# A window-attention and spectral-mixing kernel: where in the start of the first image the weights of queries, keys and values are loaded and prepared

## The chip, the cores and the metric

The kernel runs on one core of a Trainium2 chip. The metric is device time in microseconds (us) of one execution. A core has five engines that run beside one another: TensorE (PE; its weight loads are listed apart as PEld), VectorE (DVE), ScalarE (ACT), GpSimd (POOL) and SyncE (SP, which only issues transfers here). ACT and POOL also issue transfers. All data are 32-bit floats.

## The reference, cut to what matters

The input x has 8 images of 384 channels and 64 x 64 pixels. Two layers are applied, each as x + f(group norm of x):

```python
x = x + layer0(_gn(x), ...)     # layer norm over channels, then window attention
x = x + layer1(_gn(x), ...)     # 1x1 conv, 8x8 FFT filter, 3x3 depthwise conv, gate, 1x1 conv
...
xt = (xt - mu) / jnp.sqrt(var + EPS) * norm_g + norm_b
qkv = (xt @ qkv_w + qkv_b)
```

The group norm needs the mean and variance of 32 channel groups over a whole image, so no pixel can be normalised before the whole image has been read. The layer norm then needs, for every pixel, the mean over channels and the mean of the squares. Its gain `norm_g`, its shift `norm_b` and its subtraction of the mean need not touch the pixels: they can be folded into the weights of queries, keys and values and into their biases, once per launch. What is left per pixel is one factor, 1/sqrt(var + eps).

## The kernel before, in words

Each image is cut into 8 strips of 8 pixel rows (512 pixels); a strip is a tile of 128 partitions x 3 x 512, since 384 channels are 128 partitions x 3. Per image and strip, the kernel normalises (`group_normal`, L328), squares (`ln_square`, L333), sums over channels on PE with a matrix of 1/384 (`ln_sums`), makes the factor per pixel (L347 to L352), sends it through DRAM to spread it over all partitions (L356 and L358, issued on ACT's queue for the first two strips of image 0), scales the strip (`ln_scale`, L363), and then runs the matmuls for queries and keys (`pq`), values (`pvv`), scores (`pS`), and so on.

**The squares.** `ln_square` squares all three channel thirds on ACT; POOL then adds the second and the third to the first (L335, two instructions), so that `ln_sums` needs 12 matmuls for the mean and only 4 for the squares. A matmul of 32-bit floats is two passes, so the profile shows 24 and 8.

**The order of work.** A plan lists every piece with a place in time (`at(place, piece, ...)`) and the program is written in the order of the places. PE's instructions keep exactly that order (L62), as do those handed to `keep_in_program_order`; a scheduler may move the others among themselves within an engine. `fetched` and `FETCHES` count PE's instructions, and from image 1 on `small_tiles` puts empty PE instructions in so that the runs of small 64 x 64 matmuls stand at a chosen place modulo 256.

**The start, image 0.** SP issues all 8 strips of image 0 first (L92), then the constants (L95), the two halves of the raw query and key weights (L113), the value weights `wv`, the projection weights and the rest (L119 to L123). Each transfer takes one of eight semaphores in turn, and has to wait until the last transfer with that semaphore has landed. POOL issues 64 small transfers for the position tables (L171), then clears the borders (L285, L286), and only then reaches its other work. DVE takes the statistics of each strip as it lands (`strip_stats`, L237); `input_mean` and `input_std` make the mean and the standard deviation, with one small matmul each (`pm_a`, `pv_a`).

Then the weights are prepared, in pieces that stand among the layer norm of strips 0 and 1:

- `pack_qk` (L135) copies the query and key weights into their final order, 26 blocks: 20 on DVE, 6 on POOL.
- `qk_weights(0)` and `qk_weights(1)`, one per branch: 9 matmuls `pb` fold the shift into the biases (L211, L214), then `centre`.
- `v_weights`: 12 matmuls `pv` do so for the values (L223), then `centre`.
- `centre` multiplies by the gain (L198, three instructions), sums over channels with 3 matmuls `pc`, and subtracts the mean from the weights (L202).

The first matmul that uses the result is `pq` of strip 0.

Of the kernel before, what the change touches and what calls it, by code (L numbers as in the profile page):

```python
# [9 lines left out]
ALU = mybir.AluOpType  # L10
AX = mybir.AxisListType

P = 128
KC = 3
C = 384
# [3 lines left out]
NS = SW // WS  # L19
# [19 lines left out]
def block_kernel(ctx: ExitStack, tc: tile.TileContext, out, x, consts, fsel, wqk, wv, bqk, bv,  # L39
                 wp, bp, lng, lnb, rpb1, rpb2, w_in, w_dw, w_out, filt):  # L40
    nc = tc.nc
# [8 lines left out]
    def psum(name):  # L50
        return ps.tile([P, ST], F32, tag="gemm", name=name)
# [9 lines left out]
    def matmul(*args, **kw):  # L61
        tc.keep_in_program_order(nc.tensor.matmul(*args, **kw))  # L62
        fetched["count"] += 4

        n = min(fetched["empty"], fetched["share"])
        for _ in range(n):
            tc.keep_in_program_order(nc.tensor.nop(hint="empty"))
        fetched["empty"] -= n
        fetched["count"] += n
# [5 lines left out]
    def strip(tag, bufs, name):  # L75
        return sb.tile([P, KC, ST], F32, tag=tag, bufs=bufs, name=name)

    def row512(tag, bufs, name):
        return sb.tile([P, ST], F32, tag=tag, bufs=bufs, name=name)

    def rows_of(img, s):

        return img[:, s * WS:(s + 1) * WS, :].rearrange("(p k) h w -> p k (h w)", k=KC)

    first_x = []
    for s in range(NS):
        tag, bufs = ("x", 5) if s < 5 else (("xn", 1), ("ow", 1), ("y2", 1))[s - 5]  # L90
        t = strip(tag, bufs, f"x_first{s}")
        nc.sync.dma_start(out=t, in_=rows_of(x[0], s))  # L92
        first_x.append(t)
    cst = cp.tile([P, N_CONST], F32, name="cst")
    nc.sync.dma_start(out=cst, in_=consts)  # L95
    ident = cst[:, C_ID:C_ID + P]
# [12 lines left out]
    wqk_sb = cp.tile([P, KC, 6, P], F32, name="wqk_sb")  # L109
    raw_qk = []  # L110
# [4 lines left out]
    wv_sb = cp.tile([P, KC, C], F32, name="wv_sb")  # L115
    wp_sb = cp.tile([P, KC, C], F32, name="wp_sb")
    wi_sb = cp.tile([P, KC, C], F32, name="wi_sb")
    for dst, src in ((wv_sb, wv), (wp_sb, wp), (wi_sb, w_in)):
        nc.sync.dma_start(out=dst, in_=src)  # L119
    wo_sb = cp.tile([P, 2, C], F32, name="wo_sb")  # L120
    nc.sync.dma_start(out=wo_sb[:, 0, :], in_=w_out[0:P])
# [3 lines left out]
    blocks = []  # L125
# [2 lines left out]
        blocks += [(1, 96, 16, 1, 1, 32), (1, 112, 16, 1, 1, 96)] if j == 1 else [(j, 96, 32, 1, 1, c)]  # L128
    by_branch = wqk_sb.rearrange("p k (b j) c -> p k b j c", b=2)

    def pack_qk():
        for br in range(2):
            for i, (j, to, n, t, hp, of) in enumerate(blocks):
                eng = nc.gpsimd if br and i % 2 else nc.vector
                eng.tensor_copy(by_branch[:, :, br, j, to:to + n], raw_qk[t][:, :, br, hp, of:of + n])  # L135

    vec = cp.tile([P, 18], F32, name="vec")
    lng_sb, lnb_sb = vec[:, 0:3], vec[:, 3:6]
    bqk_sb, bv_sb, bp_sb = vec[:, 6:12], vec[:, 12:15], vec[:, 15:18]
    for dst, src in ((lng_sb, lng), (lnb_sb, lnb), (bv_sb, bv), (bp_sb, bp)):  # L140
        nc.scalar.dma_start(out=dst, in_=src)
    for j, to, n, t, hp, of in blocks:
        nc.scalar.dma_start(out=bqk_sb[to:to + n].rearrange("p (b j) -> p b j", b=2)[:, :, j],
                            in_=bqk[of:of + n, 4 * t:4 * t + 4].rearrange("p (b i) -> p b i", b=2)[:, :, hp])
# [20 lines left out]
    for br, tab in ((0, rpb1), (1, rpb2)):  # L165
        raw = sb.tile([P, 2, 64], F32, tag="t2", bufs=3, name=f"rpb_raw{br}")
        raw_bias.append(raw)
        for h in range(4):
            half = slice(h % 2 * 64, h % 2 * 64 + 64)
            for y2 in range(WS):  # L170
                nc.gpsimd.dma_start(  # L171
                    out=raw[half, h // 2, y2 * WS:(y2 + 1) * WS],
                    in_=bass.AP(tab.tensor, h * 225 + y2 * 15, [[15, 8], [1, 8], [1, 8]]),
# [19 lines left out]

    bq_sb = cp.tile([P, 2, 6], F32, name="bq_sb")

    def centre(w):
        for k in range(KC):
            nc.vector.tensor_scalar(w[:, k], w[:, k], lng_sb[:, k:k + 1], None, ALU.mult)  # L198
        pc = psum("pc")
        for k in range(KC):  # L200
            matmul(pc[:, 0:C], ones_c, w[:, k], start=(k == 0), stop=(k == KC - 1))
        nc.vector.tensor_tensor(w, w, pc[:, 0:C].unsqueeze(1).to_broadcast([P, KC, C]), ALU.subtract)  # L202

    def qk_weights(br):
        pb = psum("pb")
        for j in range(3):
            for k in range(KC):
                matmul(pb[:, j:j + 1], wqk_sb[:, k, 3 * br + j, :], lnb_sb[:, k:k + 1],
                       start=(k == 0), stop=(k == KC - 1))
        own = bqk_sb[:, 3 * br:3 * br + 3]  # L210
        tc.keep_in_program_order(nc.vector.tensor_tensor(own, own, pb[:, 0:3], ALU.add))  # L211

        for i in range(2):
            nc.vector.tensor_scalar(bq_sb[:, i, 3 * br:3 * br + 3], own, pick[:, i:i + 1], None, ALU.mult)  # L214
        centre(wqk_sb[:, :, 3 * br:3 * br + 3].rearrange("p k j c -> p k (j c)"))

    def v_weights():
        pv = psum("pv")
        for lo, hi, kt, cols in ((0, P, 0, 0), (0, 64, 1, 192), (64, P, 1, 128), (0, P, 2, 256)):
            for k in range(KC):  # L220
                matmul(pv[lo:hi, kt:kt + 1], wv_sb[:, k, cols:cols + hi - lo], lnb_sb[:, k:k + 1],
                       start=(k == 0), stop=(k == KC - 1))
        nc.vector.tensor_tensor(bv_sb, bv_sb, pv[:, 0:3], ALU.add)  # L223
        centre(wv_sb)

    def out_bias():
        pp = psum("pp")
# [49 lines left out]
    def at(place, piece, *args):  # L277
        plan.append((place, len(plan), piece, args))

    xs, ys, y2s, qks, vs, os_, ots, x1s, zs = ({} for _ in range(9))  # L280
# [21 lines left out]
    def load(b, s, what):  # L302

        if b == 0 and (what == "stats" or what == "norm" and s < 3):
            xs[b, s, what] = first_x[s]
            return
        t = xs[b, s, what] = strip("x", 5, f"x_{what}_{b}_{s}")
        src = x1d[b][s] if what in ("mix", "finish") else rows_of(x[b], s)
        in_dense_work(nc.sync.dma_start(out=t, in_=src))
# [13 lines left out]
    def group_normal(b, s):  # L323
# [3 lines left out]
        for k in range(KC):  # L327
            nc.vector.tensor_scalar(by_window(y[:, k, :]), image_order(t[:, k, :]), gs[:, 0:1], gs[:, 1:2],  # L328
                                    ALU.subtract, ALU.mult)

    def ln_square(b, s):
        sq = ys[b, s, "sq"] = strip("sq", 1, f"sq_{b}_{s}")
        nc.scalar.activation(sq, ys[b, s], AF.Square)  # L333
        for k in (1, 2):
            nc.gpsimd.tensor_tensor(sq[:, 0, :], sq[:, 0, :], sq[:, k, :], ALU.add)  # L335

    def ln_sums(b, s):


        p = psum(f"ln_{b}_{s}")  # L340
        for to, t, n in ((0, ys[b, s], KC), (P, ys.pop((b, s, "sq")), 1)):
            for k in range(n):
                for j in range(4):
                    matmul(p[32 * j:32 * (j + 1), to:to + P], ones_c[:, 0:32], t[:, k, j * P:(j + 1) * P],
                           start=(k == 0), stop=(k == n - 1))
        m = sb.tile([P, 2 * P], F32, tag="lc", bufs=1, name=f"m_{b}_{s}")
        nc.scalar.copy(m, p[:, 0:2 * P])  # L347
        rc = sb.tile([P, P], F32, tag="lr", bufs=2, name=f"lr_{b}_{s}")
        nc.vector.tensor_tensor(rc, m[:, 0:P], m[:, 0:P], ALU.mult)  # L349
        nc.vector.tensor_tensor(rc, m[:, P:2 * P], rc, ALU.subtract)  # L350
        nc.scalar.activation(rc, rc, AF.Sqrt, bias=eps_t)
        nc.vector.reciprocal(rc, rc)  # L352

        line = dr.tile([4, P], F32, tag="line", bufs=4, name=f"line_{b}_{s}")
        queue = nc.scalar if b == 0 and s < 2 else nc.sync
        queue.dma_start(out=line, in_=rc[0:P:32, :])  # L356
        rs = ys[b, s, "rs"] = row512("rs", 2, f"rs_{b}_{s}")
        queue.dma_start(out=rs, in_=bass.AP(line.tensor, line.offset, [[0, P], [1, ST]]))  # L358
# [354 lines left out]
    for b in range(B):  # L713
# [4 lines left out]
            at(u, load, b, s, "stats")  # L718
            at(u + (0.5 if b else 0.05), input_stats, b, s)
        if b == 0:  # L720
            at(-3.02, pack_qk)
            at(-2.9, qk_weights, 0)
            at(-0.95, v_weights)
            at(-0.94, qk_weights, 1)
            at(-0.9, position_bias, 0)
            at(-0.5, position_bias, 1)
            at(0.2, out_bias)
            at(0.2, filter_weights)
        at(first - 5.8 if b else -8, input_mean, b)
        at(first - 5.4 if b else -7.9, input_std, b)  # L730
        for s in range(NS):
            u = first + 2 * s

            v = u - 4
            at(v - 0.84, load, b, s, "norm")
            at(v + 0.15, group_normal, b, s)
            at(v + 0.45, ln_square, b, s)
            if b:
                at(v + 0.985, small_tiles, v + 1)
            at(v + 0.99, ln_sums, b, s)  # L740
            at(v + 1.35, ln_scale, b, s)

# [5 lines left out]
            for br in range(2):  # L748
                w = u + br
# [54 lines left out]
    count, dense, empty = fetched["count"], [], [0] * len(order)  # L804
    for i, (piece, args) in enumerate(order):
        count += 4 * sum(on_pe[args[1]].values()) if piece is conv_taps else FETCHES.get(piece.__name__, 0)
        if piece in (qk_tile, project):
            dense.append(i)
        elif piece is scores:
            dense = []  # L810
        elif piece is small_tiles:
            n = (RUN_AT[args[0] % 2] - count - round(WAITS[0] * args[0] + WAITS[1])) % 256
            if n < 100:
                count += n
                for j in range(n):
                    empty[dense[j % len(dense)]] += 1
# [111 lines left out]
```

## Time and profile before

| What | Value |
|---|---|
| Median of 3 runs | 3747.22 us (3746.66 to 3749.31) |
| The profiled execution: its own time | 3747.89 us |
| Its span in the trace, on which all views stand | 3745.9 us |
| PE busy | 3638.7 us, 97% of the span |
| DVE, ACT, POOL busy | 2838.6, 2378.3, 439.2 us |
| First matmul on PE / first `pq` | 31.69 us / 77.20 us |

How to read it: the timeline has, for each group of like instructions, its start and its length, the engine, the source line, the operation, the output tile and the inputs, the shape, the count, and in brackets the idle time ahead of it and what ended that. The chain of waits follows the last work of a stretch back from releaser to releaser. The windows show the busy time of each engine in a stretch, with the instruction count in brackets, then the clock granted to PE (1.00 is full), the busy share of the 16 DMA engines and GB/s. Under `PE`, the length of a group is up to the end of its last matmul, and matmuls overlap.

### The profile page before, as it was taken

The numbers are of one execution on the slowest core, as the hardware profiler recorded it, in microseconds if no ns is written. First come the engines' busy times: TensorE is split into PE (matmuls) and PEld (weight loads), VectorE is DVE, ScalarE is ACT, GpSimd is POOL, SyncE is SP. The second block draws the span as 40 slices with busy tenths as digits, with TensorE's granted clock in tenths as the row PEclk, the third lists the DMA queues.
The fourth block names the chain that finished last, engine by engine and source line by source line (L and its number), as shares of the span: only waits on it lengthen the run. The fifth ranks groups of instructions, "written<-read, shape, count | busy, mean of one in ns | idle before, by whom it ended". The sixth has DMA issues, their size and how long they took to land.

```text
span 3745.9 us, 92754 instructions
## 1 busy us (share of the span) xinstructions
PE 3638.7 (97%) x38144; PEld 2315.4 (62%) x38144; DVE 2838.6 (76%) x4601; ACT 2378.3 (63%) x3946; POOL 439.2 (12%) x776
## 2 busy tenths in 40 slices
PE   4999999999999999999999999999999999999898
PEld 3666666666666666666666666666666666666554
DVE  4554578777887687777887778877788777777898
ACT  1766676666676576665766766666676666676442
POOL 5111011111101011101101011111111111110000
PEclk9999999999999999999999999999999999999999
DMA  4222222323322233323332322323233222222422
GB/s 121 86 83 74 91 100 100 107 90 108 118 103 83 88 133 108 116 80 116 109 113 84 117 95 100 133 80 109 99 113 109 99 88 83 100 80 82 151 102 76
DMA packets 144506, 377.32 MB, mean 101 GB/s; under 512 B 12308, under 2 KB 12900, under 8 KB 144100
## 3 DMA queue, kind: packets, MB, share of 16 engines
q1 hardware_dynamic: 139952, 370.60, 28.3%
q8 instruction: 318, 5.21, 0.6%
q0 software_dynamic: 2048, 0.15, 0.1%
q10 hardware_dynamic: 2100, 0.63, 0.1%
q14 instruction: 88, 0.72, 0.1%
HBM read 270.54 MB, written 100.79 MB: 99 GB/s over the span
## 4 chain that ended last, share of the span: by engine, by line
PE 84%; DVE 6%; ACT 4%; DMA 3%; issue 2%; POOL 0%; SPq 0%; ACTq 0%; DVEq 0%; POOLq 0%
PE pq L62 23%; PE pr L62 13%; PE pt L62 12%; PE pvv L62 12%; PE pw L62 6%; PE pS L62 3%; PE pA L62 3%; PE pz L62 3%; DVE zz L673 3%; PE pT L72 3%; PE po L72 2%; PE pf L62 2%; PE ln L62 2%; PE pc L62 1%; DMA rpb_raw<-in_rpb_dram 1%
## 5 line engine op out<-in xcount | busy, mean ns | idle before, releaser
L673 DVE SCALAR_TENSOR_TENSOR zz<-z,dw_sb,zz 128x512 f32<-128x512 f32 x1490 | 1105.9, 760 | 195.4 <-ACT zz L667 172.7
L62 PE MATMUL pq<-y,wqk_sb 128*128 128x512 f32 x2160 | 990.2, 596 | 0.0
L62 PEld LDWEIGHTS pq<-y,wqk_sb 128*128 128x128 f32 x2160 | 402.7, 190 | 456.2 <-issue 424.2
L62 PE MATMUL pt<-wi_sb,xn 128*128 128x384 f32 x1536 | 535.2, 487 | 8.1 <-DVE x_finish L706 8.1
L62 PE MATMUL pr<-oT,wp_sb 128*128 128x512 f32 x1152 | 523.1, 592 | 1.0 <-DVE oT L537 1.0
L62 PE MATMUL pvv<-wv_sb,y 128*128 128x192 f32 x2880 | 496.5, 326 | 2.5 <-ACT kcd L394 2.5
L62 PEld LDWEIGHTS pvv<-wv_sb,y 128*128 128x128 f32 x2880 | 471.6, 190 | 40.1 <-issue 21.3
L394 ACT ACTIVATE qab<-pq,bq_sb,cst 96x512 f32<-96x512 f32 (+1 forms) x256 | 198.0, 773 | 402.9 <-PE pq L62 386.0
L62 PEld LDWEIGHTS pt<-wi_sb,xn 128*128 128x128 f32 x1536 | 286.0, 190 | 213.9 <-issue 49.0
L394 ACT ACTIVATE kcd<-pq,vec 32x512 f32<-32x512 f32 x512 | 348.9, 681 | 9.0
L62 PEld LDWEIGHTS pr<-oT,wp_sb 128*128 128x128 f32 x1152 | 211.1, 190 | 224.4 <-issue 209.7
L376 POOL COPY y<-y 128x384 f32<-128x384 f32 x112 | 100.2, 894 | 1583.1 <-PE pvv L62 1089.3
L349 DVE TENSOR_TENSOR lr<-m 128x128 f32<-128x128 f32 x64 | 19.7, 308 | 301.9 <-ACT m L347 301.8
L335 POOL TENSOR_TENSOR sq<-sq 128x512 f32<-128x512 f32 x128 | 167.8, 1311 | 637.2 <-ACT sq L333 632.2
L667 ACT ACTIVATE zz<-z,dw_sb 128x512 f32<-128x512 f32 x183 | 133.8, 733 | 166.1 <-PE pw L62 160.5
L394 ACT ACTIVATE qcd<-pq,bq_sb,cst 96x512 f32<-96x512 f32 (+1 forms) x256 | 197.3, 771 | 43.8 <-PE pq L62 40.4
L546 DVE SCALAR_TENSOR_TENSOR x_add<-pr,vec,x_add 128x512 f32<-128x512 f32 x192 | 143.4, 747 | 103.3 <-PE pr L62 101.5
L584 ACT COPY t<-pt 128x384 f32<-128x384 f32 x256 | 125.0, 488 | 141.6 <-PE pt L62 138.7
L428 ACT COPY v<-pvv 128x384 f32<-128x384 f32 x256 | 121.8, 481 | 129.7 <-PE pvv L62 129.3
L62 PE MATMUL pw<-zz,wo_sb 128*128 128x512 f32 x384 | 181.9, 610 | 0.0
L394 ACT ACTIVATE kab<-pq,vec 96x512 f32<-96x512 f32 (+1 forms) x256 | 174.4, 681 | 9.1 <-PE pq L62 7.4
L469 ACT ACTIVATE e<-e 128x1024 f32<-128x1024 f32 x128 | 135.3, 1057 | 68.2 <-DVE e L463 66.8
(139 smaller groups left out, 5272.6 us busy)
## 6 DMA issues: line engine op xcount, KB each, us to landing
x_add<-in_x_dram SPq DMA_DIRECT2D x64, 768.0 KB
x1d<-x_add SPq DMA_DIRECT2D x64, 768.0 KB
x_mix<-x1d SPq DMA_DIRECT2D x64, 768.0 KB
x_finish<-x1d SPq DMA_DIRECT2D x64, 768.0 KB
out_dram<-x_finish SPq DMA_DIRECT2D x64, 768.0 KB
x_norm<-in_x_dram SPq DMA_DIRECT2D x61, 768.0 KB
x_stats<-in_x_dram SPq DMA_DIRECT2D x56, 768.0 KB
rs<-line SPq DMA_DIRECT2D x62, 256.0 KB
```

The source lines that it names most:

```text
L62: tc.keep_in_program_order(nc.tensor.matmul(*args, **kw))
L72: tc.keep_in_program_order(nc.tensor.transpose(*args, **kw))
L335: nc.gpsimd.tensor_tensor(sq[:, 0, :], sq[:, 0, :], sq[:, k, :], ALU.add)
L349: nc.vector.tensor_tensor(rc, m[:, 0:P], m[:, 0:P], ALU.mult)
L376: nc.gpsimd.tensor_copy(dst[:, :, :, :, 0:4], src[:, :, :, :, 4:8])
L394: return nc.scalar.activation(dst[to:to + n], pq[of:of + n], AF.Identity, bias=bias[of:of + n], scale=scale)
L428: nc.scalar.copy(v[:, 2 * g:2 * g + 2, :, 0:HD], pvv[:, 0:384].rearrange("p (g h d) -> p g h d", g=2, h=4))
L469: nc.scalar.activation(e, e, AF.Exp)
L546: nc.vector.scalar_tensor_tensor(t[:, m, :], pr, bp_sb[:, m:m + 1], t[:, m, :], ALU.add, ALU.add)
L584: nc.scalar.copy(t1, pt[:, 0:C])
L667: nc.scalar.activation(zz.rearrange("p (r c) -> p r c", c=SW), z[:, 1:9, 1:SW + 1], AF.Copy, scale=dw_sb[:, m, 4:5])
L673: i = nc.vector.scalar_tensor_tensor(acc.rearrange("p (r c) -> p r c", c=SW), z[:, dy:dy + 8, dx:dx + SW], dw_sb[:, m, TAPS[tap]:TAPS[tap] ...
```

## The change

- SP's issue order: strips 0 to 3, constants, both halves of the query and key weights, `wv`, strips 4 to 7, and then the other weights.
- `pack_qk` runs wholly on DVE, in program order.
- The weights' pieces are planned before `input_mean`, between the strips' statistics. `centre` now ends with the matmuls `pc`; its subtraction is a piece of its own, `take_off`. That of branch 1 is planned later, behind the first strip's normalisation. The DVE instructions concerned keep program order.
- For strips 0 to 2 of image 0 the squares are not added on POOL; PE sums all three thirds, with 12 matmuls in place of 4. The plan's count is raised by 32 for each of these.

```diff
-    for s in range(NS):
+    def load_first(s):
...
+    for s in range(NS // 2):
+        load_first(s)
     cst = cp.tile([P, N_CONST], F32, name="cst")
...
-    for dst, src in ((wv_sb, wv), (wp_sb, wp), (wi_sb, w_in)):
+    nc.sync.dma_start(out=wv_sb, in_=wv)
+    for s in range(NS // 2, NS):
+        load_first(s)
+    for dst, src in ((wp_sb, wp), (wi_sb, w_in)):
         nc.sync.dma_start(out=dst, in_=src)
...
     def pack_qk():
         for br in range(2):
-            for i, (j, to, n, t, hp, of) in enumerate(blocks):
-                eng = nc.gpsimd if br and i % 2 else nc.vector
-                eng.tensor_copy(by_branch[:, :, br, j, to:to + n], raw_qk[t][:, :, br, hp, of:of + n])
+            for j, to, n, t, hp, of in blocks:
+                in_order(nc.vector.tensor_copy(by_branch[:, :, br, j, to:to + n],
+                                               raw_qk[t][:, :, br, hp, of:of + n]))
...
-    def centre(w):
+    means = {}
+    def centre(w, *key):
         for k in range(KC):
-            nc.vector.tensor_scalar(w[:, k], w[:, k], lng_sb[:, k:k + 1], None, ALU.mult)
+            in_order(nc.vector.tensor_scalar(w[:, k], w[:, k], lng_sb[:, k:k + 1], None, ALU.mult))
         pc = psum("pc")
         for k in range(KC):
             matmul(pc[:, 0:C], ones_c, w[:, k], start=(k == 0), stop=(k == KC - 1))
-        nc.vector.tensor_tensor(w, w, pc[:, 0:C].unsqueeze(1).to_broadcast([P, KC, C]), ALU.subtract)
+        means[key] = w, pc
+    def take_off(*key):
+        w, pc = means.pop(key)
+        in_order(nc.vector.tensor_tensor(w, w, pc[:, 0:C].unsqueeze(1).to_broadcast([P, KC, C]), ALU.subtract))
...
+    def summed(b, s):
+        return b > 0 or s > 2
     def ln_square(b, s):
...
-        for k in (1, 2):
+        for k in (1, 2) if summed(b, s) else ():
             nc.gpsimd.tensor_tensor(sq[:, 0, :], sq[:, 0, :], sq[:, k, :], ALU.add)
     def ln_sums(b, s):
...
-        for to, t, n in ((0, ys[b, s], KC), (P, ys.pop((b, s, "sq")), 1)):
+        for to, t, n in ((0, ys[b, s], KC), (P, ys.pop((b, s, "sq")), 1 if summed(b, s) else KC)):
...
-            at(-3.02, pack_qk)
-            at(-2.9, qk_weights, 0)
-            at(-0.95, v_weights)
-            at(-0.94, qk_weights, 1)
+            at(-9.64, pack_qk)
+            at(-9.54, qk_weights, 0)
+            at(-9.44, take_off, "qk", 0)
+            at(-9.43, v_weights)
+            at(-9.34, take_off, "v")
+            at(-9.33, qk_weights, 1)
+            at(-3.5, take_off, "qk", 1)
...
+        elif piece is ln_sums and not summed(*args):
+            count += 32
```

The statistics of strips 3, 4, 5, 6 and 7 are planned at -9.65, -9.55, -9.45, -9.35 and -9.25, `input_mean` at -8, and the normalisation of strip 0 at -3.85.

## The prediction

> **What bounds the kernel now.** I read the page first: PE is busy for 3638.7 of 3745.9 us, and the slices show it below nine tenths only at the start and the end. PE's idle time by releaser comes next: of 107 us, 31.7 are one wait for the statistics (`pm_a`) and 14.0 one wait of `ln` for POOL's sums of squares. So the change can matter only before the first `pq`; what it saves or loses there is passed on nearly whole, since PE is busy 19.3 to 20 us in each 20 us after it. The PE timeline from 50 us on:
>
> ```profile
> 50.46 0.66 PE L62 MATMUL ln<-sq,cst 128*32 128x128 f32 x8 [13.96 <-POOL sq L335]
> 51.05 4.00 PE L62 MATMUL pb<-vec,wqk_sb 128*128 128x1 f32 x18
> 54.91 4.33 PE L62 MATMUL pc<-wqk_sb,cst 128*128 128x384 f32 x6
> ...
> 60.82 2.17 PE L62 MATMUL pv<-vec,wv_sb 128*128 128x1 f32 x24
> ...
> 68.72 3.84 PE L62 MATMUL pb<-vec,wqk_sb 128*128 128x1 f32 x18
> 73.23 4.18 PE L62 MATMUL pc<-wqk_sb,cst 128*128 128x384 f32 x6 [0.67 <-DVE bq_sb L214]
> 77.20 8.09 PE L62 MATMUL pq<-y,wqk_sb 128*128 128x512 f32 x18
> ```
>
> PE sits for 14 us until POOL has added squares, then prepares weights for 26 us. The chain of waits says what held POOL: its own issues of the position tables.
>
> ```profile
> 41.38 5.51 POOL rpb_raw L171 x10
> ...
> 47.54 1.30 POOL sq L335
> ```
>
> The windows give the granted clock while the weights are prepared, and the transfer rate while the strips land:
>
> ```profile
> 24.00:26.00 2.00, 0.00 (x0) 0.00 (x0) 1.38 (x3) 0.00 (x0) 0.48 (x2) 1.00 1.02 278
> 26.00:28.00 2.00, 0.00 (x0) 0.00 (x0) 1.46 (x3) 0.00 (x0) 2.00 (x4) 1.00 1.02 367
> ...
> 68.00:70.00 2.00, 2.00 (x9) 1.61 (x7) 1.84 (x2) 0.00 (x0) 1.99 (x6) 0.50 0.00 0
> 70.00:72.00 2.00, 2.00 (x12) 2.00 (x11) 0.32 (x1) 0.00 (x0) 0.11 (x1) 0.50 0.10 38
> ```
>
> PE is busy for all of 66 to 72 us and yet at half clock. `pb` streams one column per weight load, and it seems not to count as work that raises the clock.
>
> **The change, step by step.** Removed from the path: POOL's two sums per strip (1.3 us each) and, with them, the wait for its 64 issues, which end at 46.9 us; the tables themselves are first needed by DVE at about 64 us below, so they stay hidden. Also removed: the weights' 26 us between `ln` and `pq`. They do not vanish; PE keeps program order, so they now stand ahead of `pm_a`, and the question is when they end.
>
> *Transfers.* The DVE timeline starts the statistics of strips 3, 4 and 5 at 15.11, 18.68 and 24.62 us, each after a wait for its transfer; strip 7 is there by 28.93. The second half of the raw weights now comes 481 + 1536 KB (2.07 MB) behind strip 3. By the mean rate of the 2 us windows from 16 to 26 us (323, 213, 276, 269, 278: 272 GB/s) that is 7.6 us, so 22.7; by what landed (1536 KB by 24.62, and 481 KB more at 272 GB/s) it is 26.4. I take 25.0. Strip 4, 576 + 768 KB later at about 330 GB/s, lands at 29.2; strips 5 to 7 at some 360 GB/s, to 35.7.
>
> *The weights' chain.* `pack_qk`: the 20 DVE copies of before took 1.22 + 1.41 = 2.63 us, so 26 take 3.4; they end at 28.5. `pb` starts after its first block, 25.6, and ends at 29.6. In DVE's changed order the statistics of strip 4 stand ahead of `pb`'s bias addition: 29.2 + 1.9 = 31.1. From there:
>
> - biases (0.1 + 0.36) and the first gain (0.42), with hand-overs 1.0; `pc` 4.2 at half clock (6 x 0.70), 2.1 at full.
> - `pv` 2.17 at full clock (24 x 0.09, the row at 60.82, windows at 1.00), 4.3 at half.
> - addition and gain 0.65; `pc` 4.2 or 2.1; `pb` 3.9 or, as 18 like matmuls `pp` at 92.89 show, 2.06.
> - addition, biases and gain 1.1; the last `pc` 4.2.
>
> All at half clock `pm_a` starts at 31.1 + 1.0 + 4.2 + 4.3 + 0.65 + 4.2 + 3.9 + 1.1 + 4.2 = 54.6. All at full clock DVE decides (strip statistics 1.9 each, `take_off` 1.35, aggregation 0.8, all in one queue) and it is 45.7. In the trace a stretch of `pc` with `ln` raised the clock for 3.4 us (60.5 to 63.9), and `pb` or `pv` let it fall. Three times a `pc` of 4 us is followed by light matmuls, so I expect about half of that relief: **`pm_a` at 50**, against 31.69 before. The statistics end at about the same time: strip 7's stand behind the last gain.
>
> [...]
>
> *From `pm_a` to `pq`.* Before, `pm_a` to the end of strip 0's normalisation is 35.80 - 31.69 = 4.1. Then the square 1.5; PE's 12 matmuls for the squares, 24 passes, 1.6 (24 passes of `ln` took 1.50 at 59.17): 7.3 with hand-overs. ACT's copy 0.4, the square of strip 1 1.5, its matmuls 1.6, copy 0.4: 11.4. On ACT's changed order the store of strip 0's factor stands behind that copy, and its reload behind strip 1's factor: square of strip 2 1.5, root 0.4, DVE's reciprocal 0.95, store 0.6: about 15. The reload lands some 3.1 later (issue 111.85, scaling of the strip 114.96 in the steady part), scaling 1.75: 20.0. DVE's `take_off` of branch 1 (1.35) and strips 1 and 2 (3 x 0.52 each) fit into the waits. So `pq` starts at 70.0.
>
> *What is then late.* PE has been idle for 8 us, so `pq` starts at half clock: at 0.50 for 3.4 to 6.8 us costs half of that, 1.7 to 3.4; I take 2.2. Before, `pq` came at 77.20 and half clock ended at 77.6: 0.3. So 72.2 stands against 77.5: 5.3 gained. Strip 2's sums lie in the dense part: 24 passes (0.86) for 8 (0.40), 0.5 lost; those of strips 0 and 1 are counted above. ACT, DVE and POOL have idle time there, so nothing else of the change is on PE's path. POOL's six copies and DVE's six more are hidden by the waits for strips. The empty instructions fall from 4538 to 4442 by the plan's own sum, and from image 2 on everything stands within 2 places of where it did: nothing.
>
> The sum: 5.3 - 0.5 = 4.8 off the profiled execution's 3747.89, so 3743.1. That execution is 0.7 over the median, so **3742.4 us**.
>
> **Bounds.** Weights at 22.7 or 26.4 in place of 25.0: 2.3 better, 1.4 worse. The chain all at half clock, `pm_a` 4.6 later. All at full clock, `pm_a` 4.3 earlier, and the stretch to `pq` 2.1 shorter, as its sums halve.
>
> **Rivals.**
>
> - *Full clock.* If the light matmuls do count, or `pc` carries the clock further, `pm_a` at 45.7, `pq` at 63.6, in effect 65.8: 11.7 - 0.5 gained, 3736. For it: the clock is full at 60.5 to 63.9 with `pv` in it. Against: 66 to 77.
> - *The chain moved, not hidden.* All at half clock: `pm_a` 54.6, `pq` 74.4, in effect 76.6: 0.4 gained, 3746.8. This is the case in which the change doesn't do what it says: the weights end after the strips, and the wait for POOL has become a wait for PE itself. For it: half clock in most rows of the preparation. Against: the 3.4 us relief after `ln` and `pc`.
> - *Slower, by instruction supply.* 64 more PE instructions before the first `pq` and 32 with strip 2 move all of image 0's small matmuls against PE's instruction stream, where no empty instructions correct it. Two of its 32 groups (`pS` and `pA`, 8 strips x 2 branches) show a gap with no releaser, 0.68 and 0.55. If the new place hits group after group at 0.7 each, it outweighs the 4.8 from 7 groups on and is slower by over 7.5 us from 18; all 30 would give 3763. Against: with strides that differ from strip to strip the places are spread before too, and two were hit.
>
> **How the numbers follow.** The forecast 0.56, full clock 0.28, moved and not hidden 0.10, instruction supply 0.06. A measurement of this kernel can tell about 0.2%, 7.5 us: faster is below 3739.7, slower above 3754.7. The forecast's own span, 3738.5 to 3746, lies to a tenth below that line: faster 0.28 + 0.06 = 0.34; same 0.50 + 0.10 = 0.60; slower 0.06. The range takes most of the full-clock case and of the moved chain: 3734.5 to 3747.5.
>
> **What would show it.** `pm_a` on PE at 47 to 53 us with `pc` of branch 1 right ahead of it; no idle time of PE on POOL; granted clock mostly 0.50 from 30 to 50; second half of the weights used by DVE at 23 to 26; `pq` at 68 to 72, its first rows at half clock. The prediction is wrong if `pm_a` waits for strip 7 rather than for PE, or if image 0's small matmuls show many gaps without a releaser.

## The result and the profile after

The changed kernel takes 3740.21 us (median of 15 runs, 3735.82 to 3744.84) where the kernel before takes 3746.0 on the same chip (15 runs, 3744.19 to 3749.31): 5.8 us less, a ratio of 0.9985 with a 95% interval of 0.9977 to 0.9992. The forecast was 4.8 us less. The profiled execution of the changed kernel took 3737.84 us, 2.4 below its median, over a span of 3735.9.

The PE timeline of the changed kernel from the first matmul to the second `pq`. Line numbers have shifted: L144 packs, L210 is the gain, L344 normalises, L353 squares, L384 scales the strip.

```profile
25.00 4.00 PE L62 MATMUL pb<-vec,wqk_sb 128*128 128x1 f32 x18 [25.00 <-DVE wqk_sb L144]
31.66 3.61 PE L62 MATMUL pc<-wqk_sb,cst 128*128 128x384 f32 x6 [2.65 <-DVE wqk_sb L210]
35.10 2.07 PE L62 MATMUL pv<-vec,wv_sb 128*128 128x1 f32 x24
...
41.48 2.07 PE L62 MATMUL pb<-vec,wqk_sb 128*128 128x1 f32 x18
44.60 3.87 PE L62 MATMUL pc<-wqk_sb,cst 128*128 128x384 f32 x6 [1.06 <-DVE wqk_sb L210]
48.30 0.28 PE L62 MATMUL pm_a<-mv_a,cst 128*128 128x1 f32 x2
...
67.17 10.41 PE L62 MATMUL pq<-y,wqk_sb 128*128 128x512 f32 x18 [8.86 <-DVE y L384]
...
85.18 2.06 PE L62 MATMUL pp<-vec,wp_sb 128*128 128x1 f32 x18
...
88.02 7.11 PE L62 MATMUL pq<-y,wqk_sb 128*128 128x512 f32 x12
```

The reader sees that `pm_a` has no bracket: it stands right behind the last `pc`, so PE, not the last strip, decides when it comes. Ahead of `pq`, nothing on PE waits for POOL any more. The first `pq` comes 10.0 us earlier than before (67.17 against 77.20), but its 18 passes take 10.41 us where they took 8.09, and a later stretch of 12 passes takes 7.11. The windows of the same kernel give the reason, the granted clock, in the third column from the right:

```profile
38.00:40.00 2.00, 2.00 (x4) 1.08 (x4) 2.00 (x5) 0.00 (x0) 1.24 (x3) 0.50 0.59 130
42.00:44.00 2.00, 1.54 (x14) 1.46 (x14) 1.42 (x4) 0.00 (x0) 2.00 (x5) 1.00 0.11 3
46.00:48.00 2.00, 2.00 (x5) 1.02 (x4) 1.70 (x3) 0.00 (x0) 1.89 (x21) 0.50 0.14 4
...
70.00:72.00 2.00, 2.00 (x4) 0.91 (x3) 1.95 (x5) 0.00 (x0) 2.00 (x6) 0.50 0.00 0
72.00:74.00 2.00, 2.00 (x6) 0.78 (x5) 0.00 (x0) 1.52 (x2) 0.06 (x1) 0.98 0.00 0
...
90.00:92.00 2.00, 2.00 (x3) 0.68 (x3) 0.00 (x0) 0.02 (x1) 0.00 (x0) 0.50 0.00 0
```

PE is busy for the whole of four of these six windows at half clock. By the clock's own events it goes 1.00 at 34.52, 0.50 at 37.94, 1.00 at 41.35, 0.50 at 44.76, 1.00 at 48.18 and 0.50 at 51.59: slices of 3.41 us, raised after a `pc`, fallen after a group of one-column matmuls. Ahead of the first event (34.52 here, 60.53 in the profile of before) the windows print 1.00 for want of a record: `pb` takes 4.00 us there, as at half clock, and 2.07 at full.

After the start, the first `pS` stands at 81.41 against 89.12 (7.7 earlier), the second group of `pS` is 5.6 earlier, as the slow stretch of `pq` and strip 2's longer sums lie between them, and the third to the fourteenth all stand 6.5 earlier. The two spans differ by 10.0 us. Some of the rest is gaps without a releaser in `pS` and `pA`: by the groups they sum to 4.3 us in the profile of before and 2.0 in this one. The medians, 5.8 apart, are the comparison to use.

### The profile page after: what moved, and what is told of

It is laid out like the page before. It is cut to its first block, busy times and chain, and to the rows that moved or that the text cites. A ratio compares the mean times of both kernels' runs of the same rounds, so it can differ in the third digit from the quotient of the medians.

```text
span 3735.9 us, 92749 instructions
## 1 busy us (share of the span) xinstructions
PE 3639.3 (97%) x38192; PEld 2315.4 (62%) x38192; DVE 2838.1 (76%) x4607; ACT 2375.8 (64%) x3946; POOL 431.5 (12%) x764
## 4 chain that ended last, share of the span: by engine, by line
PE 84%; DVE 7%; ACT 4%; DMA 3%; issue 2%; SPq 0%; ACTq 0%; DVEq 0%
PE pq L62 23%; PE pr L62 13%; PE pt L62 12%; PE pvv L62 12%; PE pw L62 6%; PE pS L62 3%; DVE zz L694 3%; PE pA L62 3%; PE pz L62 3%; PE pT L72 3%; PE po L72 2%; PE pf L62 2%; PE ln L62 2%; PE pc L62 1%; DMA rs<-line 1%
## 5 line engine op out<-in xcount | busy, mean ns | idle before, releaser
L370 DVE TENSOR_TENSOR lr<-m 128x128 f32<-128x128 f32 x64 | 18.7, 291 | 304.3 <-ACT m L368 304.3
L356 POOL TENSOR_TENSOR sq<-sq 128x512 f32<-128x512 f32 x122 | 159.6, 1308 | 626.3 <-ACT sq L353 621.5
```

## The experiments

The theory put to the test had three parts: PE's weight chain ahead of `pm_a` sets the new time; one-column matmuls let the clock fall; POOL's sums were the wait that mattered before. The rival was that the gain belongs to one half of the change alone, and that the other half does nothing or takes some of it back. The runs were made on three chips, where the kernel before took 3746.13 us (experiments 1 to 4), 3745.11 (5 to 8) and 3746.34 (9, 10 and the second run of 1); a difference of about 1 us to the changed kernel's 3740.21 says nothing by itself.

**1. The squares alone.** The kernel before with this edit only, in `ln_square`, `ln_sums` and the count:

```diff
+    def summed(b, s):
+        return b > 0 or s > 2
...
-        for k in (1, 2):
+        for k in (1, 2) if summed(b, s) else ():
...
-        for to, t, n in ((0, ys[b, s], KC), (P, ys.pop((b, s, "sq")), 1)):
+        for to, t, n in ((0, ys[b, s], KC), (P, ys.pop((b, s, "sq")), 1 if summed(b, s) else KC)):
...
+        elif piece is ln_sums and not summed(*args):
+            count += 32
```

> The kernel before with the squares of strips 0 to 2 of image 0 summed on PE, and nothing else of the change. Theory: the wait for POOL is worth as much by itself as the whole change, because PE is then free for the weights at 39 us instead of 51 while the strips still land first. ln of strip 0 ends near 39, the weights follow for 26 to 28 us as before, pq at 65 to 68 with the clock already full, some 10 us under the kernel before and about 3 us under the changed kernel. Rival: moving the weights is what gains, and the squares alone give 3 us or less.

Measured: 3729.08 us (5 runs, 3725.66 to 3729.21), ratio to before 0.9952 (0.9939 to 0.9964): 17 us less, not 10, and 11 less than the whole change. It was run once more, beside experiments 9 and 10:

> The squares alone once more, on the chip of the two runs beside it: the yardstick for them, and a second measurement of the version that has been the fastest. 3727 to 3731, that is 0.994 to 0.996 of the kernel before.

Measured: 3725.38 us (5 runs, 3724.16 to 3729.38), ratio 0.9946 (0.9934 to 0.9959), 21 us less. The PE timeline of this second run:

```profile
31.63 0.58 PE L62 MATMUL pm_a<-mv_a,cst 128*128 128x1 f32 x2 [31.63 <-DVE mv_a L244]
...
37.21 1.51 PE L62 MATMUL ln<-sq,cst 128*32 128x128 f32 x24 [0.86 <-ACT sq L337]
38.65 4.00 PE L62 MATMUL pb<-vec,wqk_sb 128*128 128x1 f32 x18
42.51 3.99 PE L62 MATMUL pc<-wqk_sb,cst 128*128 128x384 f32 x6
...
47.89 2.17 PE L62 MATMUL pv<-vec,wv_sb 128*128 128x1 f32 x24
50.93 2.17 PE L62 MATMUL pc<-wv_sb,cst 128*128 128x384 f32 x6 [0.87 <-DVE wv_sb L198]
52.94 2.06 PE L62 MATMUL pb<-vec,wqk_sb 128*128 128x1 f32 x18
55.72 3.49 PE L62 MATMUL pc<-wqk_sb,cst 128*128 128x384 f32 x6 [0.71 <-DVE bq_sb L214]
59.00 8.31 PE L62 MATMUL pq<-y,wqk_sb 128*128 128x512 f32 x18
```

`pm_a` stands where it stood (31.63, before 31.69). `ln` of the squares waits 0.86 for ACT, not 14 for POOL, so `pb` starts at 38.65 and not 51.05: 12.4 us, the part that I had in my figure. But from `pb` to `pq`, with the same groups in the same order, it is 20.4 us and was 26.2: another 5.8. Two rows of before, from its PE timeline, and two from its DVE timeline, tell where they come from:

```profile
63.05 0.91 PE L62 MATMUL pc<-wv_sb,cst 128*128 128x384 f32 x2
66.00 2.93 PE L62 MATMUL pc<-wv_sb,cst 128*128 128x384 f32 x4 [2.04 <-DVE wv_sb L198]
```

```profile
63.23 1.31 DVE L350 TENSOR_TENSOR lr<-m,lr 128x128 f32<-128x128 f32 x1
64.47 1.81 DVE L198 TENSOR_SCALAR wv_sb<-wv_sb,vec 128x384 f32<-128x384 f32 x2
```

POOL adds strip 2's squares from 63.13 to 65.73, and in that time DVE's `lr` takes 1.31 us (0.28 elsewhere) and two gains 1.81 (0.74 elsewhere). So PE waits 2.04 us in the middle of `pc`, where it waits 0.87 ahead of it with the squares alone: 1.2 of the 5.8. Most of the rest is the clock: the values' `pc` loses 1.7 to it, `pb` 1.8 and the last `pc` 0.7. In the kernel before the clock falls at 63.94; with the squares alone it stays at 1.00 from 46.19 to 56.42, three slices on end, and `pb` takes 2.06 for 3.84. That POOL's sums cost this part too is not shown: the clock falls at 63.94 just as the wait begins (the two passes of `pc` ahead of it end at 63.96), and experiment 9 has no such sums and loses the clock in the same groups. Together the 12.4 and the 5.8 make the 18.2 us between `pq` at 77.20 and at 59.00, and the groups of `pS` from the third to the fourteenth stand 18.45 earlier. So the weights needn't be moved for POOL's cost to go, and moving them costs 11 to 15 us.

**2. Everything but the squares.** The changed kernel with POOL's sums back:

```diff
     def summed(b, s):
-        return b > 0 or s > 2
+        return True
```

> The changed kernel with the squares summed on POOL as before. Theory: pm_a comes at 48 us, after POOL has ended its issues at 47, so POOL costs only its own sums: 1.7 us at strip 0 and again at strip 1, pq at 70 to 71.5, and 0.5 is won back at strip 2: 3 us over the changed kernel. Rival: the squares on PE are the gain, and without them the time goes back to that of the kernel before, 6 us more.

Measured: 3741.6 us (11 runs, 3739.13 to 3744.16), ratio 0.9988 (0.9979 to 0.9996), 1.4 over the changed kernel. The PE timeline shows both waits on POOL back, and how little they matter there:

```profile
56.27 0.66 PE L62 MATMUL ln<-sq,cst 128*32 128x128 f32 x8 [3.80 <-POOL sq L356]
...
61.48 0.65 PE L62 MATMUL ln<-sq,cst 128*32 128x128 f32 x8 [3.27 <-POOL sq L356]
68.85 9.91 PE L62 MATMUL pq<-y,wqk_sb 128*128 128x512 f32 x18 [6.71 <-DVE y L384]
```

With `pm_a` at 48.23, POOL is done with its issues (at 46.6 in this run) before a square exists. The same edit is worth 17 to 21 us where the sums of squares come at 37 and about 1.4, no more than the intervals of the two ratios, where they come at 53: a wait is worth what it holds back in that very order.

**3. Branch 1 and the values later.** The changed kernel with two of the three groups prepared behind the first `ln`:

```diff
-            at(-9.34, take_off, "v")
-            at(-9.33, qk_weights, 1)
-            at(-3.5, take_off, "qk", 1)
+            at(-3.5, take_off, "v")
+            at(-0.96, qk_weights, 1)
+            at(-0.6, take_off, "qk", 1)
```

> The changed kernel with two pieces moved: branch 1's weights behind the sums of strip 1, and the subtraction from wv behind the first normalisation. Theory: PE's weight chain decides pm_a, so it comes at 43 instead of 48; branch 1's weights run in PE's idle stretch ahead of pq, and their dense pc leaves the clock at full when pq starts. pq at 61 to 63 and 6 to 7 us under the changed kernel, 3733 to 3735. Rival: the strips or DVE decide pm_a, or branch 1's weights now delay pq: no gain.

Measured: 3734.77 us (6 runs, 3730.32 to 3736.92), ratio 0.9969 (0.9957 to 0.998), 5.4 less than the changed kernel. The total came as expected; its parts did not. `pv` ran at half clock this time (3.63 us, not 2.07) and `pm_a` came at 46.23 rather than 43, where it waited for DVE's aggregation and not for PE's chain; `pq` came at 64.84 but started at half clock (18 passes in 10.09 us), which I had not expected behind a `pc`.

```profile
46.23 0.35 PE L62 MATMUL pm_a<-mv_a,cst 128*128 128x1 f32 x2 [0.95 <-DVE mv_a L260]
```

**4. Strips first.** The changed kernel with the transfers in the order of before:

```diff
-    for s in range(NS // 2):
+    for s in range(NS):
         load_first(s)
...
     nc.sync.dma_start(out=wv_sb, in_=wv)
-    for s in range(NS // 2, NS):
-        load_first(s)
```

> The changed kernel with SP's order of before: all eight strips first, then constants and weights. Theory: the weights land at 35 instead of 24.7, DVE stands at the first copy with the statistics of strips 4 to 7 queued behind it, and pm_a comes at 56 to 58, pq at 74 to 77: 8 us over the changed kernel and 2 over the one before. Rival: the transfers are hidden anyway, and the order on SP makes no difference.

Measured: 3748.29 us (11 runs, 3745.98 to 3749.13), ratio 1.0005 (0.9996 to 1.0014), 8.1 over the changed kernel. As expected: the chain ahead of `pm_a` starts when the raw weights land, whatever the strips do.

```profile
33.95 4.00 PE L62 MATMUL pb<-vec,wqk_sb 128*128 128x1 f32 x18 [33.95 <-DVE wqk_sb L142]
...
58.18 0.45 PE L62 MATMUL pm_a<-mv_a,cst 128*128 128x1 f32 x2
...
77.17 10.71 PE L62 MATMUL pq<-y,wqk_sb 128*128 128x512 f32 x18 [8.82 <-DVE y L382]
```

**9. Only the transfers moved.** The squares alone, with the transfers in the order of the changed kernel, and the weights prepared in their old places (numbers as in the order of the runs):

```diff
+    for s in range(NS // 2):
+        load_first(s)
...
+    nc.sync.dma_start(out=wv_sb, in_=wv)
+    for s in range(NS // 2, NS):
+        load_first(s)
-    for dst, src in ((wv_sb, wv), (wp_sb, wp), (wi_sb, w_in)):
+    for dst, src in ((wp_sb, wp), (wi_sb, w_in)):
```

> The squares alone, with the transfers in the order of the changed kernel: the weights are loaded amid the strips, but prepared in their old places. Theory: of the 11 us by which the changed kernel is slower than the squares alone, a part is the transfers' (2.07 MB ahead of strip 4), the rest the chain on PE ahead of pm_a. Strip 7 then lands at 35.7 in place of some 30.4, DVE's statistics end at 38.4, pm_a at 38 to 39.5 in place of 33.17, and everything behind it is shifted by as much: pq at 65.5 to 67 and the time 5 to 6 us over that of the squares alone, 3734 to 3735. If the clock of the preparation falls to half as in the run with only the first weights, up to 4 more: 3738. Rival (the transfers cost nothing, all 11 are the chain's): 3729.

Measured: 3741.61 us (11 runs, 3734.9 to 3743.24), ratio 0.9984 (0.9975 to 0.9993). That is 16 us over the squares alone on the same chip, where I expected 5 to 6, at most 9. First its DVE timeline, then its PE timeline:

```profile
38.44 1.88 DVE L244 BATCH_NORM_STATS2 st<-x_first 128x6 f32<-128x512 f32 x3 [0.48 <-DMA x_first<-in_x_dram]
40.35 0.80 DVE L251 BATCH_NORM_AGGREGATE mv_a<-st 128x2 f32<-128x144 f32 x1
```

```profile
41.21 0.59 PE L62 MATMUL pm_a<-mv_a,cst 128*128 128x1 f32 x2 [41.21 <-DMA wo_sb<-in_w_out_dram]
...
61.37 3.71 PE L62 MATMUL pc<-wv_sb,cst 128*128 128x384 f32 x6 [0.87 <-DVE wv_sb L205]
...
68.68 4.18 PE L62 MATMUL pc<-wqk_sb,cst 128*128 128x384 f32 x6 [1.70 <-DVE wqk_sb L205]
72.66 8.91 PE L62 MATMUL pq<-y,wqk_sb 128*128 128x512 f32 x18
```

The last strip's statistics begin at 38.44, about when `pb` starts with the squares alone (38.65): `pm_a` comes at 41.21, 9.6 later (8.0 after the first run's 33.17), and not 5 to 6. Its bracket names a transfer, but the aggregation it needs ends at 41.15, as close ahead of it as with the squares alone (31.58 and 31.63). Up to `pq` another 4.1 are lost, 1.0 of them DVE (the wait of 1.70) and the rest the clock, full for two single slices (57.64 to 61.05 and 64.47 to 67.88) where it was three on end, so that `pc` takes 3.71 and 4.18 where it took 2.17 and 3.49. `pq` loses 0.6, and 12 later passes of it, again at half clock, 1.5 (6.89 against 5.42). That is 15.8 of the 16. They are the rows of one execution, of 3741.67 us: eight of the eleven took 3740.1 to 3743.2, but three took 3734.9 to 3736.4, which is 9.5 to 11 over the squares alone.

Four kernels now form a square. All have PE's sums of the squares; medians in us:

| | weights prepared in the old places | prepared between the statistics |
|---|---|---|
| strips loaded first | 3729.1 and 3725.4 | 3748.3 |
| weights loaded amid the strips | 3741.6 | 3740.2 |

Each half of the move alone makes the kernel with PE's sums slower, by 12 to 16 us and by 19 to 23. Made together, they are still 11 to 15 slower than neither.

**5. Only the first weights amid the strips.** The changed kernel with just branch 0's weights between the statistics, and `wv` behind the strips:

```diff
-    nc.sync.dma_start(out=wv_sb, in_=wv)
...
-    for dst, src in ((wp_sb, wp), (wi_sb, w_in)):
+    for dst, src in ((wv_sb, wv), (wp_sb, wp), (wi_sb, w_in)):
...
-            at(-9.43, v_weights)
-            at(-9.34, take_off, "v")
-            at(-9.33, qk_weights, 1)
-            at(-3.5, take_off, "qk", 1)
+            at(-0.95, v_weights)
+            at(-0.95, take_off, "v")
+            at(-0.94, qk_weights, 1)
+            at(-0.94, take_off, "qk", 1)
```

> The changed kernel, but only branch 0's query and key weights are prepared between the statistics. The values' and branch 1's weights go back to their old places, and the transfer of wv_sb goes behind the strips. Theory: what the change loses against the squares alone is the part of the weights' chain that pushes pm_a beyond the strips. With wqk_raw alone amid the strips these end some 1.6 us earlier (0.58 MB at 360 GB/s) than in the changed kernel, and DVE's last statistics decide: pm_a at 37 to 40, not 48.3. Then, as in the run with the squares alone, PE's chain behind ln decides: pm_a to the end of the first ln 7.3, the second ln about 2.5 later, then pv, pc, pb, pc in 12.4: pq at 59 to 62, about that run's 60.79. Median 3727 to 3731, that is 9 to 13 less than the changed kernel. Rival (it is the squares' sums or the clock that lose the 11 us, not the place of the weights): no better than 3738.

Measured: 3737.19 us (11 runs, 3733.64 to 3743.66), ratio 0.9978 (0.997 to 0.9987). A miss: `pm_a` came at 39.92 as said, but `pq` at 68.30, not 59 to 62. The PE timeline of the preparation:

```profile
49.67 2.17 PE L62 MATMUL pv<-vec,wv_sb 128*128 128x1 f32 x24
53.29 4.21 PE L62 MATMUL pc<-wv_sb,cst 128*128 128x384 f32 x6 [1.45 <-DVE wv_sb L209]
57.29 3.84 PE L62 MATMUL pb<-vec,wqk_sb 128*128 128x1 f32 x18
64.33 4.18 PE L62 MATMUL pc<-wqk_sb,cst 128*128 128x384 f32 x6 [3.20 <-DVE wqk_sb L209]
```

The same four groups, `pv` to the last `pc`, took 11.1 us with the squares alone (47.89 to 59.00) and take 18.6 here. Compared with those rows, `pc` loses 2.0, `pb` 1.8 and the last `pc` 0.7 to the clock, 4.5 in all, which fell at 52.08 after a single slice. The largest other part is the wait of 3.20 (0.71 there): DVE scales strip 1 (1.75 us at 61.24) in front of the biases and gains that `pc` needs. So the clock, 4.5 us here, is a part of what the squares alone win, beside the earlier `pm_a` (8.3: 31.63 against 39.92).

**6. PE busy ahead of `pq`.** Extra work only, in the changed kernel, and counted in the plan:

```diff
+    def warm():
+        pw = psum("warm")
+        for i in range(9):
+            matmul(pw[:, 0:C], ones_c, wi_sb[:, i % 3], start=(i == 0), stop=(i == 8))
...
+            at(-0.87, warm)
```

> The changed kernel with 9 extra matmuls of 384 columns (ones by wi_sb, into a PSUM tile that nothing reads), placed in PE's idle stretch of 8.9 us ahead of the first pq: extra work only. Theory: pq starts at half clock because PE was idle before it. The nine take 3.4 us at half clock and some 4.2 at full, end at about 66, ahead of the scaling of strip 0, and leave the clock at 1.00: the first 18 passes of pq take 8.1 us, not 10.4, so 2.3 less than the changed kernel, 3738, if the later half-clock slice near 90 us stays. Rival (the first rows of pq are slow for another reason, such as operands or instruction supply): pq still takes 10.4 and nothing is gained, 3740. Rival (the extra matmuls delay pq): up to 2 more.

Measured: 3737.29 us (11 runs, 3735.57 to 3740.81), ratio 0.9981 (0.9972 to 0.999), 2.9 less than the changed kernel, or 2.0 when each is taken against the kernel before on its own chip (7.8 and 5.8 less). The intervals of the two ratios overlap, so the gain is read from the rows. The PE timeline:

```profile
61.23 7.85 PE L62 MATMUL warm<-wi_sb,cst 128*128 128x384 f32 x18
70.16 7.99 PE L62 MATMUL pq<-y,wqk_sb 128*128 128x512 f32 x18 [1.07 <-DVE y L389]
```

9 useless matmuls ahead of `pq` make it 2.4 us shorter (7.99 against 10.41). That settles that `pq` was slow because PE had been idle, and what that cost. `pm_a` came at 51.29 in this execution, 3.0 later than in the profile after, though nothing ahead of it differs; from `pm_a` to the first `pS` it is 30.7 us against 33.1.

**7. `out_bias` early.** The matmuls `pp` moved from 85 us into the same idle stretch:

```diff
-            at(0.2, out_bias)
+            at(-0.95, out_bias)
```

> The changed kernel with out_bias (the one-column matmuls pp, 18 passes, 2.06 us) moved from between rows of pq at 85 us into PE's idle stretch ahead of the first pq. Theory: the one-column matmuls pp are what lets the clock fall for one slice near 90 us, at 1.7 us. Then both go: 2.06 + 1.7 less, 3736.5, and no half-clock slice at 86 to 93. Rival (the slice depends on pf's wait or on when pq began, not on pp): only the 2.06 go, 3738, and a half-clock slice still stands near 90.

Measured: 3739.29 us (11 runs, 3737.78 to 3741.41), ratio 0.9985 (0.9976 to 0.9994): 5.8 less than the kernel before, as the changed kernel, where I expected 3.7 more. PE's rows, then DVE's:

```profile
63.55 4.00 PE L62 MATMUL pp<-vec,wp_sb 128*128 128x1 f32 x18
75.99 10.59 PE L62 MATMUL pq<-y,wqk_sb 128*128 128x512 f32 x18 [8.43 <-DVE y L384]
...
95.11 5.42 PE L62 MATMUL pq<-y,wqk_sb 128*128 128x512 f32 x12
```

```profile
67.59 0.16 DVE L248 TENSOR_TENSOR vec<-vec,pp 128x3 f32<-128x3 f32 x1 [4.25 <-PE pp L62]
...
68.07 0.28 DVE L370 TENSOR_TENSOR lr<-m 128x128 f32<-128x128 f32 x1
```

The slice at half clock near 90 us is gone (12 passes in 5.42), as the theory of the one-column matmuls said: with `pp`'s own 2.06 this gained 3.6 us, seen as the lag to the changed kernel falling from 9.0 to 5.4 between the first two groups of `pS`. But the same 3.6 were lost ahead of `pq`: from `pm_a` to `pq` it is 22.5 us against 18.9. DVE's addition of `pp` stands ahead of the factor of strip 1 in DVE's order and waits 4.25 us for PE; the factor follows late, and strip 0's reload is issued on ACT behind strip 1's store. One instruction of 0.16 us, moved, cost as much as the move gained.

**8. Without the recount.** The changed kernel without the 32 added to the count of instructions for each of the three strips:

```diff
-            count += 32
+            pass
...
-    assert fetched["count"] == count
```

> The changed kernel without the 32 added in the plan's count of instructions for each ln with three thirds of squares, so that the empty instructions stand as if PE had 96 instructions less in its stream: from image 0's end on, all small matmuls are shifted against the stream of instructions by up to 96 of 256. Theory: the count keeps image 1 and later where they were, so this term is worth something only if the shift puts groups of small matmuls on a gap; the gaps seen cost 0.7 to 0.85 each and some 2 or 3 of 32 groups of image 0 show one. With all 96 groups of the images behind hit it would be +70 us, with one in ten +7. I expect 3745 to 3765, slower than the changed kernel. Rival (the place against the stream does not matter): 3740.

Measured: 3776.74 us (4 runs, 3773.34 to 3782.05), ratio 1.0085 (1.0072 to 1.0099), 36.5 over the changed kernel and beyond what I expected. The profile is of the slowest of the four, 3782.05 us. The groups of the small matmuls on PE, first of the changed kernel, then of this one; the idle time ahead of them is behind the bar:

```profile
L62 PE MATMUL pS<-kcd,qcd 64*64 64x64 f32 x4096 | 88.3, 218 | 0.6 <-issue 0.6
```

```profile
L62 PE MATMUL pS<-kcd,qcd 64*64 64x64 f32 x4096 | 99.6, 220 | 39.4 <-issue 39.3
```

Gaps without a releaser, 0.6 us in the one and 39.3 in the other, cover the difference. The line that only counts is worth more than any other of the change: without it, the kernel is 32 us slower than before.

**10. PE busy ahead of `ln`.** The squares alone, with 5 extra matmuls in PE's idle time, counted in the plan:

```diff
+    def warm(n, s):
+        pw = psum("warm")
+        for k in range(n):
+            matmul(pw, ones_c, first_x[s][:, k], start=(k == 0), stop=(k == n - 1))
...
+            at(-8.3, warm, 3, 5)
+            at(-8.2, warm, 1, 7)
+            at(-7.8, warm, 1, 6)
```

> The squares alone, and 5 extra matmuls of 512 columns (ones by a strip, into PSUM tiles that nothing reads) in PE's idle time: three when strip 5 is there, one when strip 7 is, one between pv_a and the first ln. Theory: full clock from about 32 to 38 or longer, so the first ln takes 0.86 a half in place of 1.76 and 1.51, and if the clock outlasts ln, pb 2.06 in place of 4.00 and pc 2.1 to 3 in place of 3.85: pq 1 to 4 earlier than with the squares alone, 3725 to 3728. Rival (the clock falls again in the sparse stretch around pm_a, by 37): nothing gained, 3729, or up to 1 lost where an extra matmul stands in front of pm_a or ln.

Measured: 3730.78 us (5 runs, 3730.29 to 3734.39), ratio 0.996 (0.9948 to 0.9973), 5.4 slower than the squares alone on the same chip. The PE timeline shows both halves of why:

```profile
30.90 5.25 PE L62 MATMUL warm<-x_first,cst 128*128 128x512 f32 x8 [30.90 <-DMA cst<-in_consts_dram]
35.99 0.28 PE L62 MATMUL pm_a<-mv_a,cst 128*128 128x1 f32 x2
...
42.20 2.17 PE L62 MATMUL pb<-vec,wqk_sb 128*128 128x1 f32 x18
```

That difference is of two medians of five, and against the first run of the squares alone it is 1.7. The clock did outlast `ln`: `pb` takes 2.17 where it took 4.00. But the extra matmuls need the constants, which land behind all strips at 30.90, not strip 5 alone; so they ran for 5.25 us in front of `pm_a`, which came at 35.99 and not 31.63. I had read the wrong input of the instruction. At the first `pS` the two profiles are 2.5 us apart; the rest of their 4.9 comes later, 1.2 of it as gaps without a releaser in `pS` and `pA`, and is not explained.

## Why the prediction was right, point by point

The direction and the size came out: 4.8 us forecast, 5.8 measured, 3740.21 within the range. By its steps:

- **Transfers.** The second half of the weights was used at 24.72 (forecast 25.0), strip 4's statistics began at 28.95 (29.2), the bias addition of `pb` came at 30.74 (31.1). These rows move between executions: in the five profiles whose program is the same up to there (the changed kernel and experiments 2, 6, 7 and 8), strip 4's statistics begin at 28.78 to 31.51.
- **The chain on PE, `pm_a` at 50.** In the profile after it is 48.30: I gave the clock half of its relief, and in that execution each of the three `pc` raised it for a whole slice, so that `pv` and `pb` behind a `pc` both ran at full clock (2.07 each). Others were less lucky: in experiment 7 the first `pc` did not raise it, and `pv` took 3.61. From the first `pc` to `pm_a`, 17.9 by the forecast (50 less 32.1), the five profiles took 16.6, 16.7, 18.7, 19.2 and 19.6, and `pm_a` lies at 48.23, 48.30, 51.29, 53.03 and 53.48, on the mean 50.9. Half of the relief was a middle between two bounds, not worked out from when the clock rises; that it met the mean within 1 us is in part luck. That PE and not the last strip decides, with no bracket on `pm_a`, was right in all five.
- **From `pm_a` to `pq`, 20.0.** 18.9 in the profile after, 19.0 in experiment 8. The chain of store, reload and scaling went as written.
- **`pq` at half clock, 2.2 lost.** 2.3 by its rows (10.41 against 8.09), and experiment 6 takes 2.4 of it away.
- **Strip 2's sums, 0.5.** 24 passes take 0.84 where 8 took 0.40.
- **Not foreseen:** the slice at half clock near 90 us, 1.7 lost (7.11 against 5.42). Experiment 7 shows that `pp` brings it. It is there in the changed kernel and experiments 2, 3, 6, 8 and 9, and not in both runs of 1 and in 4, 5 and 10, which have `pp` too, nor in the kernel before. The count below tells them apart by how much of `pp` and `pf` falls into one slice.
- **The sum.** Two misses offset each other: the first `pS` came 7.7 earlier in the profile, not 5.3, and the slice near 90 us took 1.7 of that back. With `pm_a` moving by 5 us between executions, agreement to 1 us owes something to luck.
- **The rivals.** Full clock: no, 0.50 in three of the six slices from 31.1 to 51.6. Moved and not hidden: no, that is experiment 4 (`pq` at 77.17, no gain), which needs the strips loaded first. Instruction supply: in image 0 no group after group was hit; that the place against the stream counts, experiment 8 shows (39.3 us of gaps without a releaser), only that the count of the plan had taken care of it from image 1 on. That these gaps come from the supply of instructions was my guess and is not shown.

What the prediction didn't see is what the change gives away. It took the 14 us of POOL's wait and the 26 us of preparation as one obstacle, both to be moved. The first goes with the squares alone, and 5.8 us of the second with it. Of the 17 to 21 us that this gains, the move takes back 11 to 15: the 2.07 MB ahead of strip 4 push the statistics 8.0 to 9.6 us back (experiment 9), and the clock no longer holds for three slices on end. The step that hid this is "the weights' 26 us between `ln` and `pq`" as a cost that is removed: I priced where it went, but not what it would have been had it stayed where it was without the wait for POOL.

On the clock, the rows say: `pb`, `pv` and `pp` are work for PE, and yet the clock falls behind them (0.50 from 37.94, 44.76 and 89.14 us on, ahead of the last without idle time on PE), while a `pc` that fills most of a slice raises it for the next (1.00 from 34.52, 41.35 and 48.18). The records allow a count. For each slice of 3.41 us in the first 110 us of the thirteen profiles, add up the columns that the matmul passes stream, each pass weighted by its rows and columns as a share of 128*128, the largest that the profiles print, and take the slices ahead of the first event as half clock, as `pb` ran there: the 224 slices that half clock follows hold at most 1501, the 195 that full clock follows at least 1536. A slice of dense matmuls holds 2050 to 2190 at half clock. So it matters where a slice begins: the slices with `pp` and `pf` hold 813 to 1362 in the six profiles where the clock then fell, 1711 or more in the six where it did not; the slice of the kernel before that ends at 63.94 holds 1036, the first full slice with the squares alone (46.19 to 49.60) 1740; and in experiment 3 the `pc` ahead of `pq` lies across two slices, of 1260 and 1423. The weighting was chosen after the fact, and in the last 230 us of the kernel it parts the slices less well (full clock from 1206 on, half clock up to 1450).

## What to carry to other kernels

When a change removes a wait and also moves work, try the removal alone first: here a few lines of the diff gave 17 to 21 us, and the whole of it 6. Before loading something earlier, price what it pushes back in the same queue, and before moving a small instruction, read what stands behind it on its engine. In the start of this kernel the clock followed the work's density and made an order of matmuls worth microseconds without any engine waiting (4.5 in experiment 5); look at the granted clock beside every row whose length has changed.

## What the runs showed of the hardware

- The granted clock moves in slices of 3.41 us, and groups of matmuls that stream one column per weight load let it fall, also where PE is busy without a break (0.50 from 89.14 behind `pp` in the profile after). In the start of this kernel it follows the columns streamed in the slice before, with the border between 1501 and 1536. Dense matmuls whose result nobody reads raised it too: behind them `pq` took 7.99 us and not 10.41 (experiment 6), and `pb` 2.17 and not 4.00 (experiment 10).
- Where the runs of 64 x 64 matmuls stand against PE's instruction stream is worth 36 us here: 39.3 us of gaps without a releaser for a shift of 96 instructions.
- Beside POOL's sums some of DVE's operations took longer, in the profile of before: 1.35 and 1.31 us for two `lr` of 0.28, which begin at 54.57 and 63.23, within POOL's additions (53.02 to 55.78 and 63.13 to 65.73), and 1.81 for two gains of 0.37, at 64.47. Taking the additions away took the slow rows away (`lr` 0.28 to 0.38 in experiment 1, second run). Not all were slowed: a gain at 54.23, within the additions too, took 0.42. What tells them apart is not shown.
- The landing of the same transfers moves by up to 2.7 us from execution to execution (strip 4 in five profiles), and `pm_a` behind them by 5.3. The runs of the changed kernel spread over 9 us, those of before over 5.
- 2.07 MB ahead of the last four strips push the statistics back by 8.0 and 9.6 us (experiment 9 against the two runs of 1), which is 257 and 216 GB/s, slower than the 272 that I had read from the windows of before; with landings that move by 2.7 us, these are rough figures.
